# Which rows take the third parts' square sums of an attention layer, and where they stand in TensorE's order

## The chip, the core and the metric

The kernel runs on one core of one Trainium2 chip. The metric is the device time of one execution in microseconds (us). It is launched once with all its inputs in device memory; everything is float32.

## What is computed

The program has four layers on an image batch of 8 x 16 x 128 x 128. The change touches the first one alone, an attention layer over tokens of 3 parts with 48 numbers each, of which every pixel has one:

```python
x = _fold_to_kernels(in_x)                       # (pixels, T=3, 48)
h = _ln(x)
q, k, v = jnp.split(h @ w_attn.T, 3, axis=-1)    # 4 heads of 12
att = softmax(q k / sqrt(12));  y = att v
x = x + y @ w_attn_proj.T
h = _ln(x)
x = x + gelu(h @ w_fc.T) @ w_fc_proj.T
x = _ln(x)
x = jnp.sum(x, axis=1);  out = conv_w x + conv_b
```

So there are three norms: one of the input, one after the attention (below: the second), one after the two dense layers (the last). Each needs, for every part of every token, the sum of the squares of 48 centered numbers. The three layers that follow are a gated 1x1 convolution, a rational convolution and a spline convolution.

## The kernel before

**Tiles.** A step handles four rows of all eight images: 512 pixels of each image in the free dimension, and two images on the partitions at a time (48 numbers of one in rows 0 to 47, of the other in rows 64 to 111). Such a pair of images has the number `k` (0 to 3). The halves `d` of a step are the pairs 0 and 1 (`d` = 0) and the pairs 2 and 3 (`d` = 1); `u` (0 to 2) is the part of the token. There are 32 steps.

**Overlap of steps.** The loop at line 656 is software-pipelined. In round `n`, four or five steps are at work: `ahead` (step n+2) is centered, `then` (n+1) gets its queries, keys, values, scores and softmax, `new` (n) gets its attention outputs, its second norm and most of the dense layers, `old` (n-1) finishes its dense layers and its last norm, and `done` (n-2) is stored.

**The order of TensorE.** All its matmuls in this layer go through `pe` (line 360), which chains each to the one before, so TensorE works in exactly the order in which the code issues them. (A float32 matmul shows as two MATMUL rows in the profile; "x12" is six matmuls.) A round begins with twelve `attend` calls (slots 0 to 11), for pair `k = i // 3` and shift `j = i % 3`: three matmuls write the spread weights to PSUM banks 1 to 3, VectorE multiplies them with the values (line 518), and for `j` > 0 GpSimd adds the product to the pair's sum (line 527). Banks 1 to 3 exist once, so the next `attend` waits for VectorE. After every slot the code issues what the list `between` holds for it (lines 664 to 705), and this fills TensorE meanwhile: the rest of old's dense layers in slots 0 to 6, projections of the first half in 7 and 8, centering, and the next step's queries, keys and values. After the twelve slots come the second half's projections, queries, the norm's sums, then `narrow`, the scores, and the units of the dense layers, with the softmax of `then` in between (lines 705 to 753). The next round's first `attend` needs this softmax's result (VectorE, line 509).

**Square sums.** `square` (line 540) makes the squares of a half, one tile per part, on ScalarE. `vary` (line 546) sends them through TensorE: for each of three parts and two pairs, one matmul with a selector of 32 columns sums the 48 squares of both images and adds them into two rows of PSUM bank 0. All norms of a round share this bank. It is used as four sets of 32 rows; `place(k, u)` (line 369) says which set takes a sum, and which rows of it. Matmuls of 32 columns that go to different sets can run at the same time; those of one set follow one another. `Variances` (line 372) counts the sums still due in each set, to close the accumulation, and `finish` (line 392) turns the bank into 1/sqrt with three ScalarE and two VectorE instructions. `normed` (line 598) and `finish` of the step read a sum back through selectors (`bcast`, `last`) that follow the same placing. A round adds 4 sums for `ahead` (one in each set), 12 for `new`, 12 for `old`.

**Pools.** Square tiles, hidden tiles and some others come from the pool "work" with 11 buffers (line 342), used in turn; a buffer is free once the last reader of its earlier tile is done. PSUM results other than the attention's come from pairs of banks, given out in turn by `two` (line 336): banks 4 to 7 in the twelve slots, banks 2 to 7 after them.

Of the kernel before, what the change touches and what calls it, by code (L numbers as in the profile page):

```python
# [33 lines left out]

def _constants():
    g, r = (a.reshape(-1) for a in np.mgrid[0:2, 0:E])
    token = 64 * g + r
    h, c = r // HD, r % C  # L40
    parts = {}
    center = np.zeros((128, 64))
    center[token, r] = 1.0
    center[token, :E] -= 1.0 / E
    parts["center"] = center

    halfvar = np.zeros((128, 62))
    halfvar[token, 30 + g] = -0.5 / E
    parts["halfvar"] = halfvar
    score = np.zeros((128, 56))  # L50
    score[token, 24 + 4 * g + h] = 1.0
    parts["score"] = score
    spread = np.zeros((128, 4, 128))
    bcast = np.zeros((128, 5, 128))
    last = np.zeros((128, 3, 128))
    for t in range(4):
        bcast[32 * t + 16 + g, 4, token] = 1.0
        for n in range(4):
            bcast[32 * t + 4 * (n // 2) + 2 * (n % 2) + g, n, token] = 1.0
            spread[32 * t + 8 * n + 4 * g + h, n, token] = 1.0  # L60
    for k in range(4):
        for u in range(3):
            v = 32 * (2 * (k % 2) + u % 2) + 8 + 4 * (u // 2) + 2 * (k // 2)
            last[v + g, u, 32 * k + 16 * g + c] = 1.0
    parts["spread"] = spread.reshape(128, 512)
    parts["bcast"] = bcast.reshape(128, 640)
    parts["last"] = last.reshape(128, 384)
    p = np.arange(BC)
    parts["pair"] = 0.5 * (p[:, None] // 2 == p[None, :] // 2)


    parts["chan"] = 1.0 * (p[:, None] % 4 == np.arange(4)[None, :])
    gather = np.zeros((128, 2, 2, 32))
    for g in range(2):
        gather[p, 0, g, g * 16 + p % C] = -1.0
        gather[p, 1, g, g * 16 + p % C] = 2.0
    parts["gather"] = gather.reshape(128, 128)
    parts["image"] = 1.0 * (p[:, None] // C == np.arange(B)[None, :])
    parts["basis"] = 3 * (3.5 - (p // C)[:, None])

    copies = np.zeros((128, 2, 128))
    for g in range(2):
        for j in range(8):
            copies[p, g, j * C + p % C] = p // C % 2 == g
    parts["copies"] = copies.reshape(128, 256)
    at, where = 0, {}
    for name, a in parts.items():
        where[name] = (a.shape[0], at, at + a.shape[1])
        at += a.shape[1]
    out = np.zeros((128, at), np.float32)  # L90
    for name, a in parts.items():
        n, lo, hi = where[name]
        out[:n, lo:hi] = a
    return out, where


_CONST, _WHERE = _constants()


@with_exitstack  # L100
def kernel(
# [132 lines left out]
    with ExitStack() as l0:  # L234
        wp = l0.enter_context(tc.tile_pool(name="w0", bufs=1))
        with tc.tile_pool(name="x0", bufs=2) as xp:
# [6 lines left out]
            mean0, _, rs0, d0 = group_stats(bn0, "0")  # L243
# [123 lines left out]
                    pe(p[o : o + 64, k], w(k)[r : r + 64], src[r : r + 64, k], start=start, stop=True)  # L367

        def place(k, u):
            return 32 * (2 * (k % 2) + u % 2), 4 * (u // 2) + 2 * (k // 2)  # L370

        class Variances:

            def __init__(self, first, others):
                self.due = [first + n * others for n in (4, 2, 4, 2)]
                self.begun = [False] * 4

            def add(self, t, c, sq):  # L380
# [22 lines left out]
        class Step:  # L403
# [139 lines left out]
                for u in range(3):  # L543
                    nc.scalar.activation(self.sq[d][u], self.x2[d][:, u], AF.Square)  # L544

            def vary(self, d, m, var):
                for u in range(3):
                    for k in range(2):
                        t, c = place(2 * d + k, u)
                        var.add(t, 8 * m + c, self.sq[d][u][:, k])  # L550
# [47 lines left out]
            def normed(self, i):  # L598
                d, u = divmod(i, 3)
                p = two()  # L600
                for k in range(2):
                    t, _ = place(2 * d + k, u)
                    w = bcast[t : t + 32, 2 * (u // 2) + d]
                    pe(p[:, k], w, self.r2[t : t + 32], start=True, stop=True)
                self.h2 = work("h2")
                nc.vector.tensor_mul(self.h2, p, self.x2[d][:, u])  # L606
# [38 lines left out]
        def end(gen):  # L645
            for _ in gen:
                pass
# [5 lines left out]
        def step(n):  # L653
            return steps.get(n)

        for n in range(-2, NCH + 3):
            if n + 2 < NCH:
                steps[n + 2] = Step(4 * (n + 2))
            done = steps.pop(n - 2, None)
            new, old, then, ahead = step(n), step(n - 1), step(n + 1), step(n + 2)  # L660
            var = Variances(int(bool(ahead)), int(bool(new)) + int(bool(old)))


            between = [[] for _ in range(12)]

            def put(i, f, *a):
                between[i].append(lambda: f(*a))

            if old:
                put(0, old.square, 0)  # L670
                u4, u5 = old.unit(4), old.unit(5)
                for i, gen in enumerate((u4, u4, u4, u5, u5, u5)):
                    put(i, next, gen, None)
                put(5, old.vary, 0, 1, var)
                put(6, old.back, 5)
                put(6, old.square, 1)
            if done:
                put(2, done.store)
            if new:
                put(7, new.project, 0, 0)  # L680
                put(7, new.project, 0, 1)
                put(8, new.project, 0, 2)
                put(8, new.square, 0)
            if ahead:
                put(8, ahead.center, 0)
            if then:
                put(9, then.scaled, 0)
            if old:
                put(9, old.vary, 1, 1, var)
            if then:  # L690
                put(10, then.qkv, 0)
                put(11, then.scaled, 1)
            if ahead:
                put(11, ahead.center, 1)
            if new:
                put(11, new.vary, 0, 0, var)
            if ahead:
                for d in range(2):
                    ahead.load(d)
            ring["from"] = 2 if new else 1  # L700
            for i, fs in enumerate(between):
                if new:
                    new.attend(i // 3, i % 3)
                for f in fs:
                    f()
            ring["from"] = 1
            if new:
                for u in range(3):
                    new.project(1, u)
                new.square(1)  # L710
            if then:
                then.multiply(0)
                then.qkv(1)
                then.multiply(1)
            if ahead:
                ahead.first(var)
            if new:
                new.vary(1, 0, var)
            if any((new, old, ahead)):
                r = var.finish()  # L720
                for s, name in ((ahead, "r1"), (new, "r2"), (old, "r3")):
                    if s:
                        setattr(s, name, r)
            if old:
                end(old.narrow())
            if then:
                then.scores(0, range(4))
            if new:
                new.normed(0)
            if then:  # L730
                then.scores(1, range(4))
            if new:
                end(new.unit(0))
            if then:
                then.scores(0, (4,))
                then.scores(1, (4,))
                then.scores(2, range(5))
            if new:
                end(new.unit(1))
            if then:  # L740
                then.scores(3, range(5))
            soft = then.softmax() if then else iter(())
            next(soft, None)
            if new:
                end(new.unit(2))
            if old:
                old.finish()
            end(soft)
            if new:
                end(new.unit(3))  # L750
# [13 lines left out]
    with ExitStack() as l1:  # L764
# [50 lines left out]
        for s in range(4):  # L815
            for p in range(2):
                if 0 <= s - p < 3:
                    n = slice(3 * (s - p), 3 * (s - p) + 3)
# [10 lines left out]
        mean, dm, rs, _ = group_stats(bn1, "1")  # L829
# [84 lines left out]
    with ExitStack() as l2:  # L914
# [3 lines left out]
        mean, _, rs, _ = group_stats(bn2, "2")  # L918
# [219 lines left out]
    with ExitStack() as l3:  # L1138
        wp = l3.enter_context(tc.tile_pool(name="w3", bufs=1))
        tmp = l3.enter_context(tc.tile_pool(name="tmp3", bufs=2))  # L1140
        mean, _, rs, d = group_stats(bn3, "3")
# [48 lines left out]
        v = tmp.tile([128, 1024], F32, name="v", bufs=4)  # L1190
# [294 lines left out]
```

## Time and profile before

| | us |
|---|---|
| median of 3 runs | 10728.44 (10727.74 to 10730.07) |
| the profiled execution | 10728.63 |
| its span, first to last instruction | 10726.8 |
| first attention round to the end of this layer, about | 195 to 3420 |
| rest: the other three layers | 3430 to 10726 |
| one round, first `attend` to the next round's | 99.65 to 103.04 |

The profile page gives the busy time of each engine over the span, then the span in 40 slices; this layer is slices 2 to 13. Other answers of the trace list instructions in order of time (start, duration, engine, line, tile written <- tiles read, shape, count; in brackets how long the engine sat idle before and what ended that), the chain of waits that ended last, and the busy time of each engine in any stretch that one asks for, with the granted TensorE clock (PEclk, 1.00 is full speed). Times in them count from the span's start.

### The profile page before, as it was taken

To read this page: it belongs to the slowest core of one execution; us is meant where nothing else is said; L and a number is where in the kernel's file an instruction comes from. 1 tells how busy PE (TensorE), PEld (TensorE's weight loads), DVE (VectorE), ACT (ScalarE), POOL (GpSimd) and SP (SyncE) were. 2 spreads that over 40 slices of the span, in tenths; PEclk is the share of its full clock that TensorE was granted. 3 is DMA by queue.
4 is the path that set the end of the run, shared out by engine and by line. 5 is a ranking of instruction groups with operands and counts; after the bars stand their busy time and mean duration, and the time that the engine had idled before them with its cause. 6 is when DMAs were issued, how large, how long until landed. Compare 5 with 4: busy or idle time off the path is not lost.

```text
span 10726.8 us, 191623 instructions
## 1 busy us (share of the span) xinstructions
PE 9016.0 (84%) x81588; PEld 2440.6 (23%) x81588; DVE 8720.1 (81%) x6829; ACT 8613.6 (80%) x7107; POOL 5545.4 (52%) x2681
## 2 busy tenths in 40 slices
PE   4999999999998568888888888888888888888799
PEld 1222222222222112222222222222222222222222
DVE  3555555555555569999999999999999999999977
ACT  2555555555554679999999999999999999999988
POOL 3655655555553555555555555555555555555522
PEclk8999999999999789999999999999999999999999
DMA  1000000000001320000000000000000000000022
GB/s 50 14 14 12 16 13 14 15 13 13 16 10 44 96 87 8 14 7 8 14 8 7 14 8 8 14 7 8 14 8 8 14 8 7 14 8 8 7 62 61
DMA packets 189456, 205.04 MB, mean 19 GB/s; under 512 B 46776, under 2 KB 155448, under 8 KB 186552
## 3 DMA queue, kind: packets, MB, share of 16 engines
q1 hardware_dynamic: 179944, 190.68, 6.7%
q8 instruction: 641, 10.50, 0.4%
q10 hardware_dynamic: 8656, 2.11, 0.1%
q14 instruction: 215, 1.76, 0.1%
HBM read 107.15 MB, written 60.04 MB: 16 GB/s over the span
## 4 chain that ended last, share of the span: by engine, by line
DVE 42%; PE 24%; issue 21%; ACT 7%; POOL 3%; DMA 2%; SPq 1%; ACTq 0%; DVEq 0%; POOLq 0%
PE banks L360 18%; DVE u L1030 15%; DVE pn L1030 10%; DVE u L1034 8%; DVE y L518 2%; DVE t L1020 2%; PE pn L971 2%; PE pd L971 2%; PE acc L1334 1%; POOL y L527 1%; DVE x L538 1%; ACT u L152 1%; DMA yd<-y 1%; ACT hid L152 1%; SPq L1298 1%
## 5 line engine op out<-in xcount | busy, mean ns | idle before, releaser
L1043 POOL TENSOR_TENSOR v<-t,u 128x1280 f32<-128x1280 f32 x1152 | 3374.3, 2929 | 2990.1 <-DVE t L1020 2960.8
L971 PE MATMUL pd<-f,wb 32*64 32x512 f32 x18432 | 2518.4, 610 | 332.8 <-ACT t L1009 301.0
L1020 DVE SCALAR_TENSOR_TENSOR t<-t,u 128x2048 f32<-128x2048 f32 x1152 | 2637.5, 2289 | 34.8 <-ACT u L152 25.2
L1009 ACT ACTIVATE t<-pd 128x1024 f32<-128x1024 f32 x2304 | 2348.6, 1019 | 86.6 <-POOL v L1043 42.3
L152 ACT ACTIVATE u<-u 128x2048 f32<-128x2048 f32 x1152 | 2200.4, 1910 | 0.0
L152 ACT ACTIVATE u<-t 128x2048 f32<-128x2048 f32 x1152 | 2192.1, 1903 | 0.0
L971 PE MATMUL pn<-f,wa 32*64 32x512 f32 x18432 | 1324.8, 624 | 938.4 <-DVE u L1034 938.1
L1030 DVE TENSOR_TENSOR u<-pn,u 128x1280 f32<-128x1280 f32 x1152 | 1718.1, 1491 | 39.4
L152 ACT ACTIVATE hid<-banks 128x1024 f32<-128x1024 f32 x576 | 571.4, 1023 | 1046.6 <-PE banks L360 1044.7
L527 POOL TENSOR_TENSOR y<-y 128x1536 f32<-128x1536 f32 x256 | 894.7, 3495 | 830.9 <-DVE y L518 830.9
L1062 PE MATMUL acc<-u,const 128*32 128x512 f32 (+2 forms) x13824 | 1118.9, 456 | 0.0
L1030 DVE TENSOR_TENSOR pn<-pn,u 128x768 f32<-128x768 f32 x1152 | 1104.2, 959 | 0.0
L1034 DVE SCALAR_TENSOR_TENSOR u<-t,pn 128x768 f32<-128x768 f32 x1152 | 1087.6, 944 | 0.0
L518 DVE TENSOR_TENSOR y<-banks,vp 128x1536 f32<-128x1536 f32 x384 | 672.9, 1752 | 274.0 <-PE banks L360 271.8
L971 PEld LDWEIGHTS pd<-f,wb 32*64 32x64 f32 x18432 | 512.1, 131 | 1610.2 <-ACT t L1009 1548.7
L1062 PE MATMUL acc<-v,const 128*32 128x512 f32 (+1 forms) x9216 | 749.9, 443 | 1.5 <-POOL v L1043 1.5
L544 ACT ACTIVATE sq<-x 128x1024 f32<-128x1024 f32 x384 | 397.9, 1054 | 412.3 <-DVE x L538 289.7
L971 PEld LDWEIGHTS pn<-f,wa 32*64 32x64 f32 x18432 | 279.5, 131 | 1947.3 <-DVE u L1034 1936.7
L470 POOL TENSOR_TENSOR pd<-q,kp 128x1536 f32<-128x1536 f32 (+1 forms) x256 | 693.6, 2733 | 8.0 <-PE banks L360 7.2
L360 PE MATMUL banks<-att,const 32*128 32x512 f32 x2304 | 497.3, 667 | 173.5 <-DVE att L509 95.9
L360 PE MATMUL banks<-h,wfc 64*128 64x512 f32 (+1 forms) x3072 | 618.4, 631 | 14.5 <-DVE h L606 14.5
L606 DVE TENSOR_TENSOR h<-banks,x 128x1024 f32<-128x1024 f32 x192 | 232.6, 1211 | 435.5 <-ACT hid L152 230.4
(182 smaller groups left out, 8068.9 us busy)
## 6 DMA issues: line engine op xcount, KB each, us to landing
f<-yd SPq DMA_DIRECT2D x512, 101.6 KB
yd<-y SPq DMA_DIRECT2D x320, 130.0 KB
xin<-in_x SPq DMA_DIRECT2D x752, 32.0 KB
four<-sil SPq DMA_DIRECT2D x256, 65.0 KB
xj<-in_x SPq DMA_DIRECT2D x8, 1024.0 KB
xl<-in_x SPq DMA_DIRECT2D x32, 256.0 KB
x1d<-xl SPq DMA_DIRECT2D x32, 256.0 KB
x<-x1d SPq DMA_DIRECT2D x8, 1024.0 KB
```

The source lines that it names most:

```text
L152: ins = nc.scalar.activation(out_, in_, func, **kw).ins
L360: in_turn("pe", mm(*args, skip_group_check=True, **kw).ins)
L470: ins = nc.gpsimd.tensor_mul(t[:, :n].rearrange("p n (a b) -> p n a b", a=4), rows(self.q[d][:, k]).unsqueeze(1).to_broadcast([128, n, 4, W]),
L518: ins = nc.vector.tensor_mul(y.rearrange("p n (a b) -> p n a b", a=4), banks[:, 1:4].rearrange("p n (a b) -> p n a b", a=4), windows(v, j, 3),
L527: in_turn("pool", nc.gpsimd.tensor_add(self.y[k], self.y[k], y).ins)
L971: yield mm(p[64 * (u % 2) : 64 * (u % 2) + 64, u // 2], w[lo : lo + 32, q % 2, n].rearrange("p c f -> p (c f)"), fs[g * NP + q][lo : lo + ...
L1009: in_turn("act", nc.scalar.activation(self.t[:, ab], self.pd, AF.Abs).ins)
L1020: ins = nc.vector.scalar_tensor_tensor(self.t, self.t, 1.0, self.u, op0=ALU.add, op1=ALU.mult).ins
L1030: in_turn("dve", nc.vector.tensor_mul(u if cols.start else p, p, u).ins)
L1034: ins = nc.vector.scalar_tensor_tensor(u, t, 2.0, p, op0=ALU.subtract, op1=ALU.mult).ins
L1043: ins = nc.gpsimd.tensor_mul(self.v, t, u).ins
L1062: ins = mm(accs[k][32 * q : 32 * q + 32, lo % 512 : (hi - 1) % 512 + 1], gather[:, int(part == 1), g], flat(c.u)[:, ab, lo:hi] if src is N ...
```

## The change

1. `place` sends the third part (`u` = 2) of the second half (pairs 2 and 3) to the other two sets. Before, parts 0, 1, 2 of a pair went to sets 0, 1, 0 for even pairs and to 2, 3, 2 for odd ones. After, the third part goes to set 0 or 2 in the first half, and to 1 or 3 in the second. Every set now gets three sums of a step, where it was 4, 2, 4, 2; the counters and the selector `last` follow.
2. `vary` takes a list of (half, part). For both `new` and `old`, it is called first with parts 0 and 1 of the first half, and later with the third parts of both halves and parts 0 and 1 of the second half.
3. For `old`, the first call stays in slot 5 (4 matmuls where there were 6). The second call (8 matmuls) is in slot 8, ahead of the last projection of the first half and the centering; before, 6 matmuls stood in slot 9 behind `scaled`.
4. For `new`, the first call stays in slot 11 (4 matmuls where there were 6), the second stays ahead of `var.finish` (8 where there were 6).

```diff
+def _set(k, u):
+    return 2 * (k % 2) + (k // 2 if u == 2 else u)
...
-            v = 32 * (2 * (k % 2) + u % 2) + 8 + 4 * (u // 2) + 2 * (k // 2)
+            v = 32 * _set(k, u) + 8 + 4 * (u // 2) + 2 * (k // 2)
...
-            return 32 * (2 * (k % 2) + u % 2), 4 * (u // 2) + 2 * (k // 2)
+            return 32 * _set(k, u), 4 * (u // 2) + 2 * (k // 2)
...
-                self.due = [first + n * others for n in (4, 2, 4, 2)]
+                self.due = [first + 3 * others for _ in range(4)]
...
-            def vary(self, d, m, var):
-                for u in range(3):
+            def vary(self, m, var, *parts):
+
+                for d, u in parts:
                     for k in range(2):
                         t, c = place(2 * d + k, u)
                         var.add(t, 8 * m + c, self.sq[d][u][:, k])
...
-                put(5, old.vary, 0, 1, var)
+                put(5, old.vary, 1, var, (0, 0), (0, 1))
                 put(6, old.back, 5)
                 put(6, old.square, 1)
             if done:
                 put(2, done.store)
+            if old:
+                put(8, old.vary, 1, var, (0, 2), (1, 2), (1, 0), (1, 1))
             if new:
                 put(7, new.project, 0, 0)
                 put(7, new.project, 0, 1)
...
             if then:
                 put(9, then.scaled, 0)
-            if old:
-                put(9, old.vary, 1, 1, var)
...
-                put(11, new.vary, 0, 0, var)
+                put(11, new.vary, 0, var, (0, 0), (0, 1))
...
-                new.vary(1, 0, var)
+                new.vary(0, var, (0, 2), (1, 2), (1, 0), (1, 1))
```

No matmul is added or left out, and no transfer is touched.

## The prediction

> **What bounds the kernel now.** The page first: which engine is full in slices 2 to 13, the attention layer.
>
> ```profile
> PE 9016.0 (84%) x81588; PEld 2440.6 (23%) x81588; DVE 8720.1 (81%) x6829; ACT 8613.6 (80%) x7107; POOL 5545.4 (52%) x2681
> PE   4999999999998568888888888888888888888799
> DVE  3555555555555569999999999999999999999977
> ```
>
> TensorE is at 90% or more there and VectorE at half; the other layers are VectorE's and untouched. But not all of TensorE's time sets the end. The chain of waits through slots 5 to 11 of one round says where it does:
>
> ```profile
> 2007.68 1.08 DVE x L630
> ...
> 2012.75 1.76 DVE y L518
> ...
> 2014.55 6.23 PE banks L360 x36
> ...
> 2024.15 1.77 DVE y L518
> ...
> 2026.05 3.46 POOL y L527
> ```
>
> The four blocks of square sums ("sq") in TensorE's rows of that round start at 2001.75 (slot 5), 2016.74 (slot 9), 2025.89 (slot 11) and 2035.24 (the end). Slots 5 and 9 lie on the chain. Slot 11 does not: behind it TensorE idles 0.74 for GpSimd's add.
>
> ```profile
> 2001.75 1.91 PE L360 MATMUL banks<-sq,const 128*32 128x512 f32 x12
> 2014.55 1.13 PE L360 MATMUL banks<-att,const 32*128 32x512 f32 x6 [0.27 <-DVE y L518]
> 2016.74 1.91 PE L360 MATMUL banks<-sq,const 128*32 128x512 f32 x12
> 2029.56 2.79 PE L360 MATMUL banks<-y,wpc 64*64 64x512 f32 x20 [0.74 <-POOL y L527]
> 2080.46 1.13 PE L360 MATMUL banks<-att,const 32*128 32x512 f32 x6 [2.67 <-DVE att L509]
> ```
>
> The last row is a second thing: once a round TensorE idles 2.67 us for the softmax. The clock changes only at multiples of 3.413 us, so I asked for the busy time in those stretches around this gap, in three successive rounds (gap ends 1980.81, 2080.46, 2181.56); PEclk stands third from the end.
>
> ```profile
> 1976.42:1979.83 3.41, 1.73 (x16) 0.31 (x8) 3.41 (x3) 1.61 (x2) 0.54 (x1) 1.00 0.00 0
> 1979.84:1983.25 3.41, 2.44 (x12) 0.99 (x14) 3.23 (x3) 2.54 (x4) 0.00 (x0) 1.00 0.00 0
> ...
> 2078.83:2082.24 3.41, 1.78 (x10) 0.71 (x12) 3.30 (x3) 2.61 (x4) 0.00 (x0) 1.00 0.00 0
> 2082.24:2085.65 3.41, 3.41 (x11) 0.98 (x10) 1.17 (x1) 2.18 (x3) 0.00 (x0) 0.50 0.00 0
> ...
> 2177.82:2181.23 3.41, 1.08 (x12) 0.15 (x4) 3.41 (x3) 2.27 (x3) 0.00 (x0) 1.00 0.00 0
> 2181.23:2184.64 3.41, 3.08 (x6) 1.00 (x6) 1.41 (x2) 1.70 (x2) 0.00 (x0) 0.50 0.00 0
> 2184.64:2188.05 3.41, 3.41 (x10) 1.19 (x8) 1.76 (x1) 1.02 (x1) 0.00 (x0) 0.50 0.00 0
> ```
>
> Where the gap is split so that no stretch is idle for much more than half, the clock stays (round one); with 1.64 us idle at a stretch's beginning the next runs at half speed (two); with 2.3 idle the next two do (three). The rounds take 99.65, 101.10 and 103.04 us, from gap end to gap end. Call phase the place of the gap's end in its stretch: 0.98, 1.64 and 0.34. 99.65 is 29 stretches + 0.66, 101.10 is 29 + 2.11, 103.04 is 30 + 0.64: each round moves the phase to the next one's, and three together are 303.79 = 89 stretches. The pattern repeats to the layer's end.
>
> **The change part by part.** Durations are this execution's. Six sums in four sets took 4, 2, 4, 2 rows, so four passes: 1.84 us to the next start (2001.75 to 2003.59). Four sums are two passes: 1.02, as other blocks of eight rows (2000.73 to 2001.75). Eight balanced sums are four passes again, 1.84.
> Slot 5: 1.84 to 1.02, but slot 6's attend needs VectorE's product, which ends 2002.77: it starts 2002.82 instead of 2003.59, 0.77 sooner. Slots 6 to 8 repeat with that shift: attend 8 at 2009.85.
> Slot 8: attend 1.07, sums 1.84 (their squares are ready: line 630 ends 2008.13, the last square 2009.3), projection 1.02, centering 1.02: attend 9 at 2014.80, where it was 2014.55. The new block is thus not hidden; it only absorbs the 0.27 idle and 0.4 of waits for VectorE in the projection and centering (2011.75 to 2014.28). One square of `new` gets its buffer from part 2 of `old`, now read in slot 8: ScalarE's 2011.0 becomes 2012.0, and its next need is the third square at 2015.2, so that wait is covered; without cover it would cost 1.0.
> Slot 9: no sums, but attend 10 now waits for VectorE: product 9 starts 2014.80 + 1.26 and takes 1.76, so 2017.87 (was 2018.58). The queries wait for `hn` behind it: 2017.73 + 1.21 + 0.05 = 2018.99 (was 2019.64): 0.65 sooner. Keys, values, attend 11, product 11 and GpSimd's add follow with the same shift, and TensorE resumes at 2028.91 instead of 2029.56.
> Slot 11: 0.82 less in front of that wait, hidden by it; the idle grows to 1.56.
> End: sets 0 and 2 had 1 + 2 + 3 + 1 sums, narrow products and scores (14 passes), the others 12; now all have 14. The last sum stays in the sixth pass. Nothing gained or lost.
> So a round at full clock is 0.65 shorter; bounds 0.50 (if every hand-over costs the 1.13 of the rows that wait) and 0.77 (if slots 8 to 10 gave nothing back). Times 31 rounds: 20 us, if the clock did as before.
>
> **What the clock does with it.** Rounds 3 to 5 (gap ends 457.77, 560.22, 662.71, 765.71) all had two slow stretches: 102.45, 102.49, 103.00. Every third is some 0.55 longer (662.71's attend takes 3.21 instead of 2.08, as its banks are still being read; the banks' turn comes round every three rounds). Full-clock rounds are then 99.65, 99.65, 100.20; mean 99.83. Two slow stretches cost 102.45 - 99.65 = 2.80 at phase 0.28, and 103.63 - 100.20 = 3.43 at -0.95 (round 2, gap end 354.14, 0.95 before the stretch's end): 0.51 less per us of phase. So if the phase runs late the round gets cheaper, if early dearer: it settles where the mean round is 30 stretches, 102.40. Before, that was at 99.83 + 2.57 = phase 0.73; the long third round threw it to 1.02, past the edge near 0.9, where the rest of the stretch is no longer idle for half (0.62 still had two slow stretches, 0.98 none). That throw won the cheap pattern of 89. Now the mean is 99.18 and 30 stretches need a price of 3.22, at phase 0.28 - 0.42 / 0.51 = -0.54, with swings of about 0.4: 1.4 from the edge. Round 2 would begin at 354.14 - 0.65 (phase 1.81), step to 0.4 or stay at -1.1, and both end in the trap. Then each round is 102.40 where the mean was 101.49 (354.14 to 3195.99 in 28).
> Sum: gap end of round 30 at the boundary 351.68 + 28 x 102.40 - 0.5 = 3218.4, before 3195.99: +22.4. Round 30 was free (99.20): two slow stretches +3.2, its own saving 1.3 (there attend 9 idled 1.71, which takes the sums whole): +1.9. Rounds 31 and 32: -0.5 each. +23.3 on 10728.63 (the median of the runs is 0.2 lower): 10752. Own range 10742 (some rounds start in the free zone, 3.4 a round for up to three) to 10764 (+1.1 for each of ten rounds that start late).
> The Trainium skill, "TensorE: Matmul & The Clock Gate", Part 1, gives free-running windows of 3413 ns and half rate only after an idle window, and advises against gaps over about 3 us. The period agrees with the rows; the threshold does not: half an idle window was enough here. By the page a 2.67 us gap is harmless, and the sum would be -20 us: 10709.
>
> **Rivals.** (1) The slow stretches keep their mean price (101.26 - 99.83 = 1.43 a round), since something with the banks' period of three sets them, not the phase: for it, the two periods coincide from round 6 on; against it, rounds 3 to 5 were all slow. 10728.6 - 20 = 10709; this side is faster, and it decides wherever the mean price rises by less than 0.65. Range 10702 to 10718. (2) The wait behind slot 11 grows from 0.74 to 1.56, and the matmuls before it fill half the array only; if that counts as less than half busy, a second slow stretch falls on the projections: 1.4 to 3.4 more in some rounds, 10765 to 10830. Against: 1.61 idle in one stretch (3242.77 on) left the clock at 1.00. (3) The block in slot 8 eats the saving (attend 9 later by over 0.8): then the old pattern stays, 10722 to 10735.
>
> **How the numbers follow.** Forecast 0.62, rival 1 0.20, rival 2 0.10, rival 3 0.08. 0.2% (21.5 us) is about what a measurement can tell from no change. The forecast lies mostly above it (0.47 slower, 0.15 same), rival 1 mostly under 10707 or close (0.15 faster, 0.05 same), rival 2 is slower (0.10), rival 3 is same (0.04), slower 0.03, faster 0.01. Faster 0.16, same 0.24, slower 0.60. Range 10704 to 10766; beside it the likeliest's own, 10742 to 10764.
>
> **What would show it.** Right: gap ends 102.4 apart with two slow stretches in nearly every round; sums x8, x16, x8 with starts 1.02, 1.84, 1.02 apart from the next block; attend 9 at +0.25, queries at -0.65; 1.5 idle behind slot 11 with PEclk 1.00. Wrong: full-clock rounds as often as before, or half clock behind slot 11.

## The result and the profile after

| | before | after |
|---|---|---|
| median, us | 10728.49 (10726.14 to 10734.18, 8 runs) | 10759.48 (10754.45 to 10766.46, 8 runs) |
| ratio to before | | 1.0029, 95% interval 1.0021 to 1.0039 |
| profiled execution | 10728.63 | 10766.46 |
| last dense matmul of the attention layer at | 3403.2 | 3435.9 |
| from that matmul to the end of the span | 7323.6 | 7328.8 |
| rounds 2 to 29, sum and mean | 2841.9, 101.49 | 2873.8, 102.64 |

The change makes the kernel 31 us slower, 0.29%. The layer that was edited ends 32.7 us later. Of the 5 us behind that matmul, 0.9 lies ahead of the next layer's first one (3420.74 and 3454.25), and 4.3 in layers that the edit does not touch. Those take 7304.9 to 7314.0 us in the twelve profiled executions of this case, and the one of after is 7 us above its median.

The page of the kernel after, busy time by engine and the slices of TensorE and its clock:

```profile
PE 8986.3 (83%) x81588; PEld 2431.0 (23%) x81588; DVE 8722.6 (81%) x6829; ACT 8610.4 (80%) x7107; POOL 5545.1 (52%) x2681
PE   4999999899998668888888888888888888888799
PEclk8999999999999889999999999999999999999999
```

The instruction counts are those of before, and TensorE is still at 90% or nearly so in this layer. The page alone does not show 31 us. TensorE's rows of one round of after do show the new order (start, duration, line, tiles, count, idle ahead of it):

```profile
2019.00 1.07 PE L364 MATMUL banks<-sq,const 128*32 128x512 f32 x8
2020.07 1.13 PE L364 MATMUL banks<-att,const 32*128 32x512 f32 x6
...
2028.17 1.92 PE L364 MATMUL banks<-sq,const 128*32 128x512 f32 x16
...
2031.90 1.13 PE L364 MATMUL banks<-att,const 32*128 32x512 f32 x6
...
2034.97 1.13 PE L364 MATMUL banks<-att,const 32*128 32x512 f32 x6 [1.09 <-DVE y L522]
2036.19 1.95 PE L364 MATMUL banks<-hn,wqkv 64*64 64x512 f32 x16
...
2042.44 1.06 PE L364 MATMUL banks<-sq,const 128*32 128x512 f32 x8
...
2046.16 2.79 PE L364 MATMUL banks<-y,wpc 64*64 64x512 f32 x20 [1.65 <-POOL y L531]
2051.84 2.78 PE L364 MATMUL banks<-sq,const 128*32 128x512 f32 x24
...
2064.49 1.09 PE L364 MATMUL banks<-h,wfc 64*64 64x512 f32 x8 [0.54 <-ACT hid L156]
```

Four of before's rows go beside them, besides those in the prediction:

```profile
2003.59 1.13 PE L360 MATMUL banks<-att,const 32*128 32x512 f32 x6
...
2019.64 1.95 PE L360 MATMUL banks<-hn,wqkv 64*64 64x512 f32 x16
...
2044.27 1.99 PE L360 MATMUL banks<-h,wfc 64*128 64x512 f32 x8 [0.41 <-DVE h L606]
...
2047.25 1.09 PE L360 MATMUL banks<-h,wfc 64*64 64x512 f32 x8
```

From the sums in slot 5 to the projections behind GpSimd's add it is 2046.16 - 2019.00 = 27.16 us; before, 2029.56 - 2001.75 = 27.81. So this stretch is 0.65 shorter. Three waits stand beside it: 1.09 ahead of attend 10 and 1.65 behind slot 11, which the prediction had, and 0.54 ahead of the second dense matmuls, which it had not. The experiments ask what each of them costs.

### The profile page after: what moved, and what is told of

Its sections match the earlier page's. It is cut to its first block, busy times and chain, and to the rows that moved or that the text cites. A ratio compares the mean times of both kernels' runs of the same rounds, so it can differ in the third digit from the quotient of the medians.

```text
span 10764.7 us, 191605 instructions
## 1 busy us (share of the span) xinstructions
PE 8986.3 (83%) x81588; PEld 2431.0 (23%) x81588; DVE 8722.6 (81%) x6829; ACT 8610.4 (80%) x7107; POOL 5545.1 (52%) x2681
## 4 chain that ended last, share of the span: by engine, by line
DVE 41%; PE 27%; issue 20%; ACT 7%; POOL 3%; DMA 2%; SPq 1%; ACTq 0%; DVEq 0%; POOLq 0%
PE banks L364 20%; DVE u L1035 15%; DVE pn L1035 10%; DVE u L1039 8%; DVE y L522 2%; PE pn L976 2%; DVE t L1025 2%; PE pd L976 2%; PE acc L1339 1%; POOL y L531 1%; ACT u L156 1%; ACT hid L156 1%; DMA yd<-y 1%; ACT L156 1%; POOL y L950 1%
## 5 line engine op out<-in xcount | busy, mean ns | idle before, releaser
L1014 ACT ACTIVATE t<-pd 128x1024 f32<-128x1024 f32 x2304 | 2348.7, 1019 | 91.5 <-POOL v L1048 44.3
```

What stands on the lines that cost most here:

```text
L1014: in_turn("act", nc.scalar.activation(self.t[:, ab], self.pd, AF.Abs).ins)
```

## The experiments

**What had to be told apart.** The full-clock rounds of after are no shorter than those of before (table below), although slots 5 to 11 gave 0.65. One reading is that ScalarE's late table load gives it back; rivals are the sums themselves and their places. Which of the moved calls makes the load late is asked of e5 and e6. And the rounds' mean grew by 1.15, so time at half clock grew; either because shorter rounds settle at multiples of a 3.413 us stretch, as predicted, or because one of the new waits brings half-clock stretches of its own.

In the table, "full clock" is the shortest round at each of the three places in the banks' turn (a dash: none there ran wholly at full clock), and "half clock" is time at PEclk 0.50 over rounds 2 to 29, parted by where it lies behind the end of the softmax gap. The last three columns are of the one profiled execution of each kernel, which can lie off the median: for after it is the slowest, for e1 the fastest.

| kernel | median, us (range, runs) | ratio, 95% interval | full clock | half clock near the gap / 33 to 44 us behind / 44 to 56 | mean round |
|---|---|---|---|---|---|
| before | 10728.49 | 1 | 99.65, -, - | 109.2 / 0 / 0 | 101.49 |
| after | 10759.48 | 1.0021 to 1.0039 | 99.63, 99.77, - | 133.1 / 44.3 / 3.4 | 102.64 |
| e1_load_early | 10729.37 (10712.86 to 10745.24, 11) | 0.9991 to 1.0009 | 99.04, 99.17, - | 92.1 / 20.5 / 0 | 101.13 |
| e2_before_filled | 10685.42 (10682.25 to 10692.65, 5) | 0.9949 to 0.9974 | 99.66, 99.80, 100.78 | 0 / 0 / 0 | 100.12 |
| e3_after_filled | 10710.03 (10702.88 to 10716.77, 11) | 0.9974 to 0.9991 | 99.64, 99.78, 100.77 | 17.1 / 34.1 / 3.4 | 100.88 |
| e4_both | 10686.77 (10681.06 to 10691.61, 5) | 0.9946 to 0.9973 | 99.03, 99.17, 100.16 | 17.1 / 17.1 / 3.4 | 100.05 |
| e5_old_only | 10729.31 (10726.15 to 10738.38, 11) | 0.9999 to 1.0017 | -, 99.48, - | 126.3 / 20.5 / 0 | 101.61 |
| e6_new_only | 10750.83 (10746.98 to 10755.72, 8) | 1.0016 to 1.0038 | 100.28, 100.42, - | 92.1 / 0 / 0 | 102.07 |
| e7_split | 10715.37 (10706.65 to 10726.97, 11) | 0.9985 to 1.0003 | -, 98.85, - | 126.3 / 0 / 0 | 100.97 |
| e8_split_load_fill | 10656.68 (10653.15 to 10659.81, 5) | 0.9926 to 0.9951 | 98.09, 98.22, - | 34.1 / 0 / 0 | 99.04 |
| e9_wait_full | 10736.57 (10733.24 to 10745.48, 11) | 1.0003 to 1.0020 | 99.64, -, - | 122.9 / 0 / 0 | 101.74 |
| e10_wait_few | 10734.64 (10730.19 to 10738.72, 11) | 1.0000 to 1.0018 | 99.63, -, - | 122.9 / 0 / 0 | 101.71 |

Each was measured beside before on its own chip; before stood at 10728.94 for e1 to e4, 10724.18 for e5 to e8 and 10726.79 for e9 and e10. Times of different groups compare to within these 5 us only.

**e1: the table load put back ahead of the wait.** ScalarE's rows of before and of after, from the copy of `z` to the first hidden tile of the round:

```profile
2040.04 1.49 ACT L357 ACTIVATE z<-banks 128x1024 f32<-128x1024 f32 x2
2041.55 1.28 ACT L152 ACT_TABLE_LOAD   x1
2045.44 1.94 ACT L152 ACTIVATE hid<-banks 128x1024 f32<-128x1024 f32 x2 [2.61 <-PE banks L360]
```

```profile
2056.67 1.49 ACT L361 ACTIVATE z<-banks 128x1024 f32<-128x1024 f32 x2
2062.12 1.28 ACT L156 ACT_TABLE_LOAD   x1 [3.96 <-PE banks L364]
2063.41 1.94 ACT L156 ACTIVATE hid<-banks 128x1024 f32<-128x1024 f32 x2
```

Before, the 1.28 us load of Gelu's table ran in the idle time and the activation waited for TensorE behind it. After, the load itself stands behind the wait, and the chain of waits of after runs through it:

```profile
2060.91 1.14 PE banks L364 x4
...
2062.12 1.28 ACT L156
...
2063.41 1.03 ACT hid L156
...
2064.49 15.15 PE banks L364 x76
```

The start of these matmuls is 3.58 us behind the first dense block (2060.91), where it was 2047.25 - 2044.27 = 2.98 before: 0.60 later. The experiment issues the load by itself ahead of the first Gelu of the phase:

```diff
+            if func == AF.Gelu:
+                begin(nc.scalar.preload_act_table_set("gelu_and_others").ins, last)
...
-                    copy(
+                    ins = nc.scalar.activation(
...
+                    phase["all"].append(ins)
```

> The changed kernel, with the activation table of the dense layers' function loaded right behind the two copies of narrow, ahead of the wait for TensorE. In the changed kernel this load stands behind that wait and costs 0.6 us of each round, so its rounds at full clock are 99.63 us and not the 99.0 that the prediction worked out. Theory 1 (the clock's stretches set the round, about 30 of them each): the round gets 0.6 shorter at full clock, but stays near 102.4 to 102.6 with slow stretches, so the time hardly moves: 10745 to 10765. Theory 2 (the load behind the wait is what made the kernel slower): 31 rounds x 0.6 = 19 us come off, 10735 to 10742, and the gap ends lie 0.6 closer.

ScalarE's rows of e1 show the load ahead of the wait again:

```profile
2130.51 1.49 ACT L568 ACTIVATE z<-banks 128x1024 f32<-128x1024 f32 x2
2132.02 1.28 ACT L157 ACT_TABLE_LOAD   x1
2135.97 1.94 ACT L158 ACTIVATE hid<-banks 128x1024 f32<-128x1024 f32 x2 [2.67 <-PE banks L366]
```

The full-clock round fell from 99.63 to 99.04 and the time by 30 us to that of before. The late load is thus a part of the loss: 0.6 a round directly, 0.6 x 31 = 19 us. The rest goes with less time at half clock (112.6 us against 180.8). But this compares e1's fastest execution, 10712.86, with after's slowest, 10766.46, so how much of it the medians hold is not shown. The theory that lets shorter rounds settle at the same length expected the time to stay and fell; the other's 19 us were too few.

**e2, e3, e4: the softmax gap filled.** Ahead of the slots, two matmuls that nobody reads stand in the 2.67 us gap: in before (e2), in after (e3), and in e1 (e4).

```diff
+            if new and old:
+                for _ in range(2):
+                    pe(banks[:, 1], last_sel[:, 0], old.r2, start=True, stop=True)
```

> The kernel before, with two matmuls that nobody reads (128 columns, into PSUM bank 1) ahead of each round's first attend, in the 2.67 us in which TensorE waits for the softmax; nothing else changes. Theory 1: they last some 1.9 us, the idle falls to about 0.8, no stretch is idle for half, and the two slow stretches a round go: rounds of 99.65, 99.65 and 100.2 us in place of a mean of 101.49, so 28 x 1.66 = 46 us off: 10675 to 10690. Theory 3 (the clock follows something else, such as the load or the banks' turn): the same time or slower, 10725 to 10760.

> The changed kernel with the same two matmuls in the softmax's wait. Theory 1: rounds of 99.63 to 99.8 us at full clock, about as the kernel before with them, if the softmax's idle is the only one that counts: 10675 to 10690. The changed kernel also has slow stretches that begin 38 to 42 us and 52 us behind the gap's end (behind attend 10 and behind slot 11); if these don't need the softmax's, some stay, at 1.4 to 1.7 us each: 10690 to 10730. Theory 3: 10755 to 10790.

> The changed kernel with the early table load and with the two matmuls in the softmax's wait. Theory 1: rounds of 99.0 us at full clock: 28 x 0.6 = 17 us less than the changed kernel with the matmuls alone, 10660 to 10675, or up to 10710 if the stretches behind attend 10 and slot 11 stay. Theory 3: 10735 to 10770.

In e2 the gap, seen in TensorE's rows, has become 0.75:

```profile
447.82 1.98 PE L360 MATMUL banks<-rstd,const 128*128 128x512 f32 x4
450.56 1.13 PE L360 MATMUL banks<-att,const 32*128 32x512 f32 x6 [0.75 <-DVE att L509]
```

No stretch of e2's rounds 2 to 29 is at half clock. One line for all of these rounds, in before and in e2 (stretch: us, busy PE, PEld, DVE, ACT, POOL, then PEclk, DMA share, GB/s):

```profile
354.00:3196.00 2842.00, 2632.14 (x14954) 731.33 (x14954) 1575.33 (x1234) 1469.61 (x1541) 1628.57 (x896) 0.98 0.06 13
```

```profile
352.00:3153.00 2801.00, 2639.36 (x15060) 737.47 (x15058) 1574.40 (x1232) 1466.48 (x1539) 1629.81 (x896) 1.00 0.05 14
```

TensorE runs more matmul rows than before (15060 against 14954) in 41 us less. So the gap alone had cost before 43 us of its time. Filling it takes 49 us from after (e3), but leaves 34 us of half clock at 33 to 44 us behind the gap: that part has a cause of its own. e4 was no better than e2, though its full-clock rounds are 0.6 shorter; it has 37.6 us of half clock left, 17.1 of them at that place.

**e5 and e6: each half of the change alone.** Both keep the new placing of the sets. e5 leaves the calls of `new` as before; e6 leaves those of `old` as before.

```diff
 e5
-                put(11, new.vary, 0, var, (0, 0), (0, 1))
+                put(11, new.vary, 0, var, (0, 0), (0, 1), (0, 2))
...
-                new.vary(0, var, (0, 2), (1, 2), (1, 0), (1, 1))
+                new.vary(0, var, (1, 0), (1, 1), (1, 2))
 e6
-                put(5, old.vary, 1, var, (0, 0), (0, 1))
+                put(5, old.vary, 1, var, (0, 0), (0, 1), (0, 2))
...
-                put(8, old.vary, 1, var, (0, 2), (1, 2), (1, 0), (1, 1))
...
+                put(9, old.vary, 1, var, (1, 0), (1, 1), (1, 2))
```

> The change for old alone: new's sums stay as before, the first half's six in slot 11, the second half's six at the end (with the new placing). Theory A (the table load waits for TensorE because new's third square is read later, which shifts the buffers of the pool): the load is free again, rounds at full clock are 99.0, 99.2 and 100.2 us as with the early load (e1), and the time is that run's, 10713 to 10745. Theory B (old's sums in slot 8 delay the load): rounds at full clock of 99.65 and the changed kernel's time, 10750 to 10770.

> The change for new alone: old's sums stay as before, six in slot 5 and six in slot 9 (with the new placing). Nothing is saved on the chain of waits, since slot 11's two passes only lengthen the idle behind them. Theory A: the load waits, so rounds at full clock are 0.6 longer than before, 100.25, 100.4 and 101.4; slow stretches only at the softmax's wait, none 36 to 44 us behind it. With the price of the slow stretches as before 31 x 0.6 = 19 us more, 10740 to 10760. Theory B: 10720 to 10735.

ScalarE's table load in e5 and in e6:

```profile
1524.29 1.49 ACT L361 ACTIVATE z<-banks 128x1024 f32<-128x1024 f32 x2
1525.80 1.28 ACT L156 ACT_TABLE_LOAD   x1
1529.69 1.94 ACT L156 ACTIVATE hid<-banks 128x1024 f32<-128x1024 f32 x2 [2.61 <-PE banks L364]
```

```profile
2044.55 1.49 ACT L361 ACTIVATE z<-banks 128x1024 f32<-128x1024 f32 x2
2050.00 1.28 ACT L156 ACT_TABLE_LOAD   x1 [3.95 <-PE banks L364]
```

With new's order as before the load is early (e5), with the new one it is late (e6, full-clock rounds 100.28). So the late load comes from `new`, whose third squares are now read later, and not from old's block: A held and B fell. The semaphores recorded with the instructions show what lies between. In before and in e5 the round's first hidden activation waits for TensorE alone, and the load in front of it for nothing, in all 30 rounds. In after and in e6 the activation waits for GpSimd as well, and the wait for TensorE stands ahead of the load, in 29 of 30; in e1 both waits stand behind the load. Why GpSimd is waited for is argued and had no run of its own: with the later readers the buffers of "work" change hands in another order, and the first hidden tile of a round gets one that GpSimd used last. e6 also has no half clock at 33 to 44 us: its slot 9 still holds old's sums.

**e7 and e8: old's eight sums split.** Four stay in slot 8, and four go into slot 9, where TensorE waits. e8 adds the edits of e1 and e2.

```diff
-                put(8, old.vary, 1, var, (0, 2), (1, 2), (1, 0), (1, 1))
+                put(8, old.vary, 1, var, (0, 2), (1, 2))
...
+            if old:
+                put(9, old.vary, 1, var, (1, 0), (1, 1))
```

> The changed kernel with old's later call cut in two: the third parts in slot 8 (4 sums), parts 0 and 1 of the second half in slot 9 (4 sums, behind scaled). Attend 9 then starts 0.8 us sooner, and the sums fill TensorE's wait ahead of attend 10. Rounds at full clock: 99.64 - 0.8 = 98.8. Theory 1 (slow stretches come from stretches in which TensorE idles or works with few rows): none any more 36 to 44 us behind the gap; those at the softmax's wait stay: 10690 to 10735. If it stays at 10750 to 10770, the wait ahead of attend 10 is not what brought the new slow stretches.

> The split of e7, the early table load of e1, and the two unread matmuls of e2 in the softmax's wait. Rounds at full clock: 99.03 - 0.8 = 98.2, 98.4 and 99.4. Theory 1: no slow stretch is left, or a few behind slot 11; the mean round is 98.7 where e2 has 100.1: 28 x 1.4 = 39 us less than e2, 10640 to 10660. If the shorter round brings slow stretches elsewhere, 10660 to 10690.

TensorE's rows of e7 from attend 9 to attend 10, without idle ahead of the latter:

```profile
1194.52 1.13 PE L364 MATMUL banks<-att,const 32*128 32x512 f32 x6
1195.63 1.13 PE L364 MATMUL banks<-rstd,const 32*128 32x512 f32 x4
1196.69 1.06 PE L364 MATMUL banks<-sq,const 128*32 128x512 f32 x8
1197.69 1.13 PE L364 MATMUL banks<-att,const 32*128 32x512 f32 x6
```

Its full-clock round is 98.85, 0.92 below after's at the same place, with the late load still in it, and no half clock is left at 33 to 44 us. e8 is 0.62% faster than before (interval 0.49 to 0.74%): it beats both kernels by more than its interval. What half clock it has left, 34.1 us, is one stretch in every third round, where the first attend takes 2.37 us (at 943.32) against 1.13 in the next round (at 1043.87).

**e9 and e10: only the wait ahead of attend 10 filled.** The kernel after with one matmul of zero weights in slot 9, with 128 rows (e9) or with 32, like attend's own (e10). It adds nothing to the sums.

```diff
             if then:
                 put(9, then.scaled, 0)
+            if new and old:
+                put(9, lambda r: pe(banks[:, 0], zeros[0:32], r[0:32], start=False, stop=False), old.r2)
```

> The kernel after, with one unread matmul more a round in TensorE's 1.09 us wait ahead of attend 10: all 128 rows of a zero weight, so it adds nothing to bank 0. Few rows count less (F): the stretch holding that wait is then mostly full-row work, the 44.3 us of half clock at 33 to 44 us behind the softmax gap go to under 10, and with about 0.4 us of round for each us the time falls by some 18 us, to 10735-10750. Busy time alone counts (B): the same. Neither (N), the half clock there has another cause: 40 us or more stay, 10750-10770.

> As e9_wait_full, but the unread matmul takes only 32 rows of the same zero weight, as attend's own matmuls do; its duration should be the same, near 1 us. F: the stretch is busy but with few rows, so the half clock at 33 to 44 us stays near 44 us and the time at 10750-10770. B: it goes as in e9_wait_full, 10735-10750. N: it stays in both.

The half clock behind attend 10 went in both, and 23 and 25 us with it (21 and 23 if each is taken against before on its own chip). In the words of these two forecasts, B (busy time) came true and F (few rows count less) fell. Two rounds with the same phase (0.42 and 0.43) and the same place in the banks' turn show it stretch by stretch, after first and then e10 (columns as above):

```profile
2233.83:2237.25 3.42, 3.42 (x32) 0.77 (x24) 3.22 (x3) 1.94 (x2) 2.92 (x2) 1.00 0.00 0
2237.25:2240.66 3.41, 2.32 (x17) 0.94 (x16) 2.65 (x3) 2.79 (x3) 2.75 (x1) 1.00 0.23 48
2240.66:2244.07 3.41, 3.41 (x18) 0.72 (x19) 2.58 (x2) 0.09 (x1) 0.00 (x0) 0.51 0.33 72
```

```profile
1908.04:1911.46 3.42, 3.42 (x35) 0.93 (x32) 3.22 (x4) 2.12 (x2) 2.91 (x2) 1.00 0.00 0
1911.46:1914.87 3.41, 3.27 (x20) 1.05 (x12) 2.65 (x3) 2.44 (x3) 3.10 (x1) 1.00 0.13 42
1914.87:1918.28 3.41, 3.08 (x22) 0.91 (x22) 2.93 (x3) 1.32 (x2) 0.29 (x1) 1.00 0.30 67
```

In after the middle stretch is busy for 2.32 us, and the next runs at 0.51. In e10 it is busy for 3.27, by this one matmul of 32 rows, and the next stays at 1.00:

```profile
1912.85 1.02 PE L366 MATMUL banks<-rstd,const 32*128 32x512 f32 x4
1913.71 1.02 PE L366 MATMUL banks<-rstd,zeros 32*128 32x512 f32 x2
1914.96 1.13 PE L366 MATMUL banks<-att,const 32*128 32x512 f32 x6 [0.24 <-DVE y L524]
```

These rounds took 104.45 and 103.33. The three of e10 that end with it, 99.63, 101.08 and 103.33, are near before's 99.65, 101.10 and 103.04.

## Why the prediction came out as it did

The measured 10759 lies in the likeliest case's own range, and the side was right. The sum behind it was not: two terms were missing and one that filled their place was wrong. A mean round of 102.40 was forecast as 99.18 at full clock and 3.22 for slow stretches; 102.64 was measured, as 100.06 (e3's mean over the three places) and 2.58. Both parts were off, in opposite directions, so it is luck that the number is so close.

- **Slots 5 to 11: right.** Slot 5's attend 0.77 sooner (2019.00 to 2020.07 against 2001.75 to 2003.59); attend 9 0.10 later (2031.90 - 2019.00 against 2014.55 - 2001.75) where 0.25 was forecast, so slot 8's block of 1.85 was not hidden, as forecast; queries 17.19 behind slot 5's sums against 17.89, 0.70 sooner where 0.65 was forecast; TensorE resumes 0.65 sooner; the wait behind slot 11 grew to 1.65 (forecast 1.56). Rival 3, slot 8 eating the saving, fell.
- **"End: ... Nothing gained or lost": wrong.** I counted passes through the sets, and they do agree: from the projections to the first dense block it is 14.75 us (2046.16 to 2060.91), before 14.71 (2029.56 to 2044.27). But with new's third squares read later, the first hidden activation waits for GpSimd too, the table load went behind the wait for TensorE, and 0.6 of the 0.65 was lost there (e1, e5, e6). "So a round at full clock is 0.65 shorter" then fails: it is 99.63 against 99.65.
- **"Attend 10 now waits for VectorE": the wait was found and its clock not priced.** It lies beside other work, so it looked free. It gives 47.7 us of half clock at and behind attend 10, the part that comes and goes with this wait (e9, e10 with it filled; e6 without it). From after to e10 the 28 rounds lose 2873.8 - 2848.0 = 25.8 us, of the 32.0 by which after exceeds before. Some of the 25.8 belongs to the gap, where the half clock fell from 133.1 to 122.9 as well. The other 6.2 go with 122.9 instead of 109.2 us of half clock near the gap.
- **"Trap" of 102.40 us in every round: the mechanism was right in part, its size was wrong.** The gap does set half-clock stretches and cost 43 us already in before (e2). But in after only 14 of 28 rounds had two near the gap, and three ran at full clock. And e1 has the full-clock rounds that the prediction had, 0.6 shorter, and takes 101.13 a round; if the 16.5 us by which its median lies above that execution all fell into these rounds, (16.5 / 28) more, 101.7, and not 102.40. The wrong step is the price: "3.43 at -0.95" came from round 2, and I carried its two slow stretches to all early phases. In after, eight rounds began at phases 2.46 to 2.65 (a stretch is 3.41, so this is -0.95 to -0.76) and had only one near the gap. The three that began a little later, 2.67 to 2.76, had two, and all three stand at the third place of the banks' turn, where round 2 stands as well. The other traces part place and phase: in the eight kernels whose gap is not filled, 55 rounds begin at phases 2.0 to 3.3; the 17 at the third place all have two stretches near the gap, and the 38 at the other places all have one. So the second stretch belongs to that place; that its longer first attend brings it is argued. The size of 3.43 was off too: it is 103.63 less 100.20, but e2 and e3, with the gap filled, take 100.78 and 100.77 at the third place at full clock. Against 100.78 it is 2.85, beside the 2.80 at phase 0.28, and little is left of "0.51 less per us of phase".
- **Rival 2** named the right mechanism at the wrong wait: behind slot 11, with 1.65 idle, there were 3.4 us of half clock; at attend 10, with 1.09, there were 44.3. **Rival 1** (mean price kept, 10709) would have needed the 0.65 and an unchanged price; with the load early and 0.6 saved (e1), the median is that of before and not 20 us under it.
- **The Trainium skill**, "TensorE: Matmul & The Clock Gate", Part 1: its window length agrees with the multiples of 3.413 us seen here. The condition in its table of the two states, an idle window, does not: the clock fell after a stretch with 2.32 us of work in 3.41. The advice in the page's "Why this matters for your kernels" against gaps of over about 3 us was not enough either: a gap of 2.67 in each round cost 43 us in all, and a wait of 1.09 some 21 to 26.

In three runs a us of half clock cost about 0.4 us of round: before (101.49 - 100.08) / 3.90 = 0.36, after (102.64 - 100.06) / 6.46 = 0.40, e10 (101.71 - 100.06) / 4.39 = 0.38. (The full-clock means are those of the three places in e2, 100.08, and in e3, 100.06.) So the change comes out as no change of the full-clock round, and (6.46 - 3.90) x 28 x 0.4 = 29 us of clock.

## What to carry to other kernels

Price an idle wait of TensorE twice, as time on the path and as a risk to the clock of the stretch behind it; the second can be all of it, and here one unread matmul of the same few rows in the wait removed it. When a reader of a pooled tile moves, look at what instructions far behind it now wait for: a new second wait put the first one in front of a table load that had been hidden. Split the time of a round into its length at full clock and its time at half clock before explaining a sum.

## What was not expected of the hardware

- A stretch with 2.32 of 3.41 us busy is followed by one at half clock (after, 2237.25), yet one with 1.73 busy is not (before, 1976.42). So busy time within the stretch, as the records show it, is not the whole rule. From 350 to 3190 us of the twelve traces, 243 stretches at full clock are followed by one at half clock and 9394 are not; the best threshold of busy time within a stretch, 1.44 us, still misjudges 122. That few-row matmuls count for less was the obvious repair, and e10 speaks against it in its plain form; that they count in part was not tried.
- The time of e1 scatters over 32 us in 11 executions, after's over 12 in 8. Half clock alone does not tell which kernel scatters: e10, with 122.9 us of it, stays within 9 in 11, and e2, with none in rounds 2 to 29, takes 10 in 5. No run here explains e1.
